# Another order of the PSUM evictions, and another dealing of the projections and linear quarters, in masked attention with an int8 linear layer

## The chip, the cores and the metric

The kernel runs on one core of one Trainium2 chip. The metric is the device time of one execution in microseconds; lower is better. The engines are named as in the profile: PE (TensorE, matmuls), PEld (its weight loads), DVE (VectorE), ACT (ScalarE), POOL (GpSimd), SP (SyncE, which here issues the DMAs).

## The reference

x has the shape 8 x 512 x 1024 (batch, channels, tokens). Attention with 16 heads of width 32 runs over the tokens, and its result, channels by tokens, goes through an int8 linear layer over the token axis; the result is added to x. Cut to what matters:

```
Q, K, V = proj(Wq), proj(Wk), proj(Wv)
att = einsum('bhqd,bhkd->bhqk', Q, K) * (1.0 / sqrt(Dh)) + b[0]
att = att * m + (1.0 - m) * NEG_INF
y = einsum('bhqk,bhkd->bhqd', softmax(att, axis=-1), V)
q, in_scale = per_token_quant_int8(y)        # rows of y: one channel, 1024 tokens
acc = einsum('bsk,nk->bsn', q, weight)       # int8, int32 sums
out = x + (acc * in_scale * w_scale[:, 0] + bias).astype(float16)
```

## The kernel before

**Groups and steps.** Four heads of one batch element make a group: 8 x 4 = 32 groups (i). A group has two halves of 512 queries (X = 2i and 2i + 1), and each half has 8 chunks of 128 keys, so a group has 16 steps, t = 0 to 15, and the kernel 512 steps s. The engines' instructions are in an order written out by hand: the loop at the end (L717 to L775) walks the steps, and each engine runs what it is given in that order.

**One step.** `scores` (L332) gives, for one chunk of keys and 512 queries, the four heads' scores: first a shift by the row's maximum (L343), then the products (L348), into two single PSUM banks and one pair. `exponentials` (L356) has ACT take the exponential in three parts (L362: two singles, then the pair). `add_up` (L365) has POOL add the exponentials of a half over its chunks (L372); for a half's first chunk (t = 0 and t = 8) it issues nothing. `maxima` (L270) computes the scores of queries by keys for a later step, `LEAD` = 11 steps ahead, to find each row's maximum: four products with 32 rows each (L281), for head j = 0 into two single banks, for head j = 1 into a pair. `take_maxima` (L289) has DVE add the mask row and reduce with a custom instruction (L301): two passes over the singles, one pass over the pair, each followed by a short read of its accumulator.

**Banks.** There are eight PSUM banks: four singles (`one`) and two pairs (`two`). `score_banks` and `maxima_banks` (L85 to L93): scores take `two[1]` and, in even steps, `one[0:2]`, in odd steps `one[2:4]`. Maxima take `two[0]` and the two singles that the scores of that step don't take. So the maxima of step s + 1 write the singles that step s used for its scores, and the pair that the maxima of step s used.

**What else PE does in a step.** After the maxima of an even step, `product` (L376) multiplies the exponentials of the last two chunks with V, into `one[0]`; `keep_product` (L384) adds that to y on DVE (L392), or, for the first pair of chunks of a half (t = 2 and 10), copies it on ACT (L390). Then a step has jobs, dealt out by `plan` (L618) and put into one bank: `one[1]` in even steps, `one[2]` in odd ones, as soon as the exponential has read it. The jobs are 24 pieces of 128 columns of the next groups' Q, K and V projections (L186), whose results ACT copies out (L219, L221, L266); four quarters of 256 columns of the linear layer of group i - 2 (L186 too), which DVE scales on the way out (L523); and the sums of the denominators (L398), copied by ACT (L404). In the kernel before, pieces come three at a time in the eight odd steps, linear quarters in steps 4, 6, 8 and 10, sums in 2 and 12.

**What follows a step.** `rest_of` (L667) spreads small work. `normalise` is four reciprocals of the denominators on DVE (L432) and then, as its last part (step number HN = 4), the product of y with them, both in SBUF (L435). For the odd half 2i - 1 it has its parts in steps 5, 6, 6, 7 and 8 of group i, for the even half 2i in steps 13, 14, 14, 15 and step 0 of the next group. `quantise` finds the row's largest value on DVE (L442, L447, L449, part 0, at step 8) and rounds in four ACT passes over y (L479, L481, L483, L485, parts 1 to 4, at steps 10, 12, 14 and 0); `turn` has a DMA transpose the result. `load_residual`, `add_residual` (POOL, L517 and L518) and the store handle the last addition for group i - 2. `split_tops` (POOL, L320 and L322) and a DMA transpose prepare the shifts three steps ahead of a half.

Of the kernel before, what the change touches and what calls it, by code (L numbers as in the profile page):

```python
# [24 lines left out]
LEAD = 11  # L25
# [8 lines left out]
def kernel(  # L34
# [15 lines left out]
    nc = tc.nc  # L50
# [3 lines left out]
    NT = T // P  # L54
    NH = T // HALF
    HN = HALF // P
    n_groups = B * NG
    n_halves = n_groups * NH
    n_steps = n_halves * NT
# [25 lines left out]
    def score_banks(s):  # L85
        a = 0 if s >= TAIL else s % 2
        return one[2 * a : 2 * a + 2], two[1 - s % 2 if s >= TAIL else 1]
# [198 lines left out]
                    stop=True,  # L286
                )

    def take_maxima(m, accs):  # L289
        X, u = divmod(m, NT)  # L290
        pair, n = divmod(u, HN)
        row = masks[X // NH // NG][0]
        if u == 0:
            tops[X] = small.tile([P, HN, HG], F32, tag="tops", name=f"tops_{X}")
        for j in range(2):
            apart = accs[j][0].tensor is not accs[j][1].tensor
            for a in range(NH if apart else 1):
                keys = slice(a * HALF, (a + 1) * HALF if apart else T)
                top = tops[X][:, n, 2 * pair + j : 2 * pair + j + 1]
                rest = work.tile([P, T], BF, tag="rest", name=f"rest_{m}_{j}_{a}")  # L300
                nc.vector.tensor_tensor_reduce(  # L301
                    out=rest[:, keys],
                    in0=accs[j][a] if apart else both(accs[j]),
                    in1=row[:, keys],
                    scale=-1.0,
                    scalar=top if a else HIGH,
                    op0=ALU.add,
                    op1=ALU.min,
                    accum_out=top,
                )  # L310
# [115 lines left out]
    def normalise(X, step):  # L426
        i, h = divmod(X, NH)
        d = dens[X]
        if step < HN:
            cols = slice(step * P, (step + 1) * P)  # L430
            source = one[2] if X == n_halves - 1 else d
            nc.vector.reciprocal(d[:, cols], source[:, cols])  # L432
        else:
            y = ys[i][:, h * HALF : (h + 1) * HALF]
            nc.vector.tensor_tensor(y, y, d, ALU.mult)  # L435
# [55 lines left out]
    def turn(i):  # L491
        _, scale, qt = quants.pop(i)
        qT = work.tile([P, NT, P], BF, tag="qT", name=f"qT_{i}")
        nc.sync.dma_start_transpose(qT, qt)
        outs[i] = qT, scale
# [92 lines left out]
    def group(i):  # L588
        return 0 <= i < n_groups
# [3 lines left out]
    def pieces(what, *args, size=P):  # L593
        multiply, keep = what
        if what is of_v:
            return [(multiply, keep, args, slice(k, k + 1), P) for k in range(NT)]
        return [
            (multiply, keep, args, slice(c, c + size), size) for c in range(0, HALF, size)
        ]
# [18 lines left out]
    def plan(i):  # L618
        if i < 0:
            early = pieces(of_qk, 0, 0, 1) + pieces(of_v, 0) + pieces(of_qk, 1, 0, 0) + pieces(of_qk, 1, 1, 0)  # L620
            return {SG - LEAD + a: early[2 * a : 2 * a + 2] for a in range(len(early) // 2)}
        steps = {}
        if i == last:
            if group(i - 2):
                steps[1] = pieces(of_linear, i - 2, 0)
                steps[3] = pieces(of_linear, i - 2, 1)
            steps[2] = [(*sums_of, (2 * i - 1,), None, HALF)]
            return steps
        k1, v, q1 = pieces(of_qk, i + 1, 1, 1), pieces(of_v, i + 1), pieces(of_qk, i + 1, 0, 1)
        q2 = pieces(of_qk, i + 2, 0, 0) if group(i + 2) else []  # L630
        k2 = pieces(of_qk, i + 2, 1, 0) if group(i + 2) else []
        row = k1 + v + q1 + q2 + k2
        for a in range(NT):
            steps[2 * a + 1] = row[3 * a : 3 * a + 3]
        if group(i - 1):
            steps[2] = [(*sums_of, (2 * i - 1,), None, HALF)]
        steps[12] = [(*sums_of, (2 * i,), None, HALF)]
        if group(i - 2):
            for h in range(NH):
                for a, piece in enumerate(pieces(of_linear, i - 2, h, size=HALF // 2)):  # L640
                    steps[4 + 4 * h + 2 * a] = [piece]
        return steps

    def job(i, t):
        if i not in plans:
            plans.clear()
            plans[i] = plan(i)
        return together(plans[i].get(t, []))
# [18 lines left out]
    def rest_of(i, t):  # L667

        if i == last:
            if t == 5:  # L670
                for step in range(HN):
                    normalise(2 * i - 1, step)
            if t == 6:
                normalise(2 * i - 1, HN)
                quantise(i - 1, 0)
            if t == 7:
                for step in range(1, 4):
                    quantise(i - 1, step)
                turn(i - 1)
            if t == 9:  # L680
                for step in range(HN):
                    normalise(2 * i, step)
            if t == 10:
                normalise(2 * i, HN)
                tops_y.append(largest(i, 0))
                for h in range(NH):
                    load_residual(i - 1, h)
        else:
            late_steps = {5: (0,), 6: (1, 2), 7: (3,), 8: (HN,)}.get(t, ())
            if group(i - 1):  # L690
                for step in late_steps:
                    normalise(2 * i - 1, step)
                if t == 8:
                    quantise(i - 1, 0)
                if t in (10, 12, 14):
                    quantise(i - 1, t // 2 - 4)
                if i == last - 1 and t == 15:
                    quantise(i - 1, 4)
                    turn(i - 1)
            for step in {13: (0,), 14: (1, 2), 15: (3,)}.get(t, ()):  # L700
                normalise(2 * i, step)
        if t == 0 and group(i - 1):
            normalise(2 * i - 2, HN)
            if group(i - 2) and i < last:
                quantise(i - 2, 4)
        if t == 1 and group(i - 2) and i < last:
            turn(i - 2)

    tops_y = []
    load_mask(0)  # L710
# [6 lines left out]
    for s in range(-LEAD, n_steps):  # L717
        i, t = divmod(s, SG)
        if i >= 2:
            h = {0: 0, 2: 1}.get(t) if i == last else {3: 0, 7: 1}.get(t)  # L720
            if h is not None:
                load_residual(i - 2, h)
            h = {2: 0, 4: 1}.get(t) if i == last else {7: 0, 11: 1}.get(t)
            if h is not None:
                add_residual(i - 2, h, nc.gpsimd)
            if t in ((4, 6) if i == last else (9, 13)):
                flush(stores)
        if t in (4, 12):
            flush(casts)
        X, u = divmod(s + 3, NT)  # L730
        if u == 0 and 0 <= X < n_halves:
            split_tops(X)
            place_tops(X)
        items = job(i, t)
        if s >= TAIL:
            items, bank = [], None
        elif s < 0:
            bank = one[2 + s % 2]
        else:
            bank = score_banks(s)[0][1 - s % 2]  # L740
        places = []
        width = 0
        for item in items:
            places.append(bank[:, width : width + item[4]])
            width += item[4]

        def multiply():
            for (what, _, args, cols, _), place in zip(items, places):
                what(*args, cols, place) if cols else what(*args, place)

        if s < 0:
            multiply()
        if s >= 0:
            scores(s)
            exponentials(s)
            add_up(s)
        m = s + LEAD
        if m < n_steps:
            maxima(m, maxima_banks(s))
            take_maxima(m, maxima_banks(s))  # L760
        if s >= TAIL:
            for a in range(ON_ARRAY if s == TAIL + 1 else s - 1, s if s > TAIL else 0):
                late(a)
        elif s > 0 and s % 2 == 0:
            acc = score_banks(s)[0][0]
            for a in (2, 1):
                product(s - a, acc, a == 2, a == 1)
            keep_product((s - 2) // NT, (s - 2) % NT == 0, acc)
        if s >= 0:
            multiply()  # L770
        for (_, keep, args, cols, _), place in zip(items, places):
            keep(*args, cols, place)
        load_ahead(i, t)
        if i >= 0:
            rest_of(i, t)  # L775
# [64 lines left out]
```

## Time and profile before

| what | value |
|---|---|
| median of 3 runs | 2576.94 us (2576.03 to 2578.45) |
| the profiled execution's own time | 2576.91 us |
| its span in the profile | 2575.1 us |
| exponential, 128x512, and 128x1024 (L362) | 684 ns, 1117 ns |
| maxima pass over a single, first and second (L301) | 682 ns, 751 ns |
| maxima pass over the pair (L301) | 1224 ns |
| addition to y (L392) | 682 ns |
| linear quarter's eviction (L523) | 479 ns |
| reciprocal (L432) | 932 ns |
| addition of exponentials on POOL (L372) | 4564 ns |

A row of the profile's groups gives the line, the engine, the operation, what is written and read, how many there are, the busy time in all and the mean of one. In the timeline, a row begins with the start and the duration in us, and brackets at its end give the engine's idle time before it and what ended that. Matmuls of different rows or columns of the array run at the same time, so that their durations overlap.

A step's length is the distance from one step's first shift product (L343) to the next one's in the timeline. For the group that starts at 1231.82 us and ends at 1310.74 us, a steady one, these starts are:

| t | 0 | 1 | 2 | 3 | 4 | 5 | 6 | 7 |
|---|---|---|---|---|---|---|---|---|
| start, us | 1231.82 | 1235.75 | 1241.38 | 1246.17 | 1251.02 | 1255.83 | 1261.01 | 1265.82 |

| t | 8 | 9 | 10 | 11 | 12 | 13 | 14 | 15 |
|---|---|---|---|---|---|---|---|---|
| start, us | 1271.34 | 1276.15 | 1281.29 | 1286.42 | 1291.24 | 1296.04 | 1301.17 | 1305.07 |

Most other groups are 78.57 us long (this one is 0.35 longer, at step 7); groups 0 and 1 take 77.50 and 77.13, group 30 takes 75.07.

### The profile page before, as it was taken

The numbers are of one execution on the slowest core, as the hardware profiler recorded it, in microseconds if no ns is written. First come the engines' busy times: TensorE is split into PE (matmuls) and PEld (weight loads), VectorE is DVE, ScalarE is ACT, GpSimd is POOL, SyncE is SP. The second block draws the span as 40 slices with busy tenths as digits, with TensorE's granted clock in tenths as the row PEclk, the third lists the DMA queues.
The fourth block names the chain that finished last, engine by engine and source line by source line (L and its number), as shares of the span: only waits on it lengthen the run. The fifth ranks groups of instructions, "written<-read, shape, count | busy, mean of one in ns | idle before, by whom it ended". The sixth has DMA issues, their size and how long they took to land.

```text
span 2575.1 us, 80820 instructions
## 1 busy us (share of the span) xinstructions
PE 2502.2 (97%) x35008; PEld 1135.4 (44%) x35008; DVE 1859.3 (72%) x3829; ACT 1524.4 (59%) x2166; POOL 2218.4 (86%) x901
## 2 busy tenths in 40 slices
PE   9999999999999999999999999999999999999997
PEld 4444444444444444444444444444444444444432
DVE  5677677777777776777777777767777777777674
ACT  1556666566666656656566665566655666555654
POOL 0998989889889889898898898898988988988992
PEclk9999999999999999999999999999999999999999
DMA  4012111121111211112111121111211122111111
GB/s 122 20 30 80 43 37 31 49 72 43 41 43 39 73 39 43 37 39 73 39 43 41 51 63 41 39 43 45 63 41 39 46 62 59 30 41 39 35 32 44
DMA packets 143509, 121.37 MB, mean 47 GB/s; under 512 B 74800, under 2 KB 108592, under 8 KB 143152
## 3 DMA queue, kind: packets, MB, share of 16 engines
q1 hardware_dynamic: 143152, 116.20, 16.5%
q8 instruction: 274, 4.49, 0.7%
q14 instruction: 83, 0.68, 0.1%
HBM read 57.70 MB, written 16.78 MB: 29 GB/s over the span
## 4 chain that ended last, share of the span: by engine, by line
PE 86%; DVE 7%; issue 4%; ACT 2%; DMA 0%; POOL 0%; DVEq 0%; SPq 0%; POOLq 0%
PE one L186 31%; PE one L281 17%; PE one L380 14%; PE one L348 13%; PE one L343 5%; DVE rest L301 5%; PE one L398 3%; DVE y L392 2%; PE two L281 2%; ACT e L362 1%; ACT den L404 1%; ACT y L481 1%; DVE tops L301 0%; DMA x<-in_x 0%; PE two L348 0%
## 5 line engine op out<-in xcount | busy, mean ns | idle before, releaser
L372 POOL TENSOR_TENSOR sum<-sum,e 128x2048 f32<-128x2048 f32 x374 | 1706.8, 4564 | 82.8 <-ACT e L362 72.9
L362 ACT ACTIVATE e<-one,kbias 128x512 f32<-128x512 f32 x1024 | 648.4, 684 | 483.1 <-PE two L348 469.7
L301 DVE CUSTOM_DVE_ANT_0 rest<-one,row 128x512 bf16<-128x512 f32 x509 | 347.3, 682 | 505.6 <-PE two L281 295.2
L301 DVE CUSTOM_DVE_ANT_0 rest<-two,row 128x1024 bf16<-128x1024 f32 x515 | 630.2, 1224 | 77.6 <-PE one L281 1.5
L362 ACT ACTIVATE e<-two,kbias 128x1024 f32<-128x1024 f32 x512 | 571.8, 1117 | 0.0
L281 PE MATMUL one<-kf,qf 32*128 32x512 f32 x1022 | 529.1, 597 | 42.0 <-DVE y L392 40.2
L281 PE MATMUL two<-kt,qt 32*128 32x512 f32 x1026 | 544.0, 613 | 0.0
L281 PE MATMUL one<-kt,qt 32*128 32x512 f32 x1014 | 539.9, 612 | 0.0
L281 PE MATMUL two<-kf,qf 32*128 32x512 f32 x1034 | 536.4, 601 | 0.2 <-DVE tops L301 0.2
L348 PE MATMUL one<-qf,kf 32*128 32x512 f32 x2048 | 524.5, 588 | 0.0
L348 PE MATMUL two<-qf,kf 32*128 32x512 f32 x2048 | 523.1, 588 | 0.0
L380 PE MATMUL one<-e,v 128*32 128x512 f32 x4096 | 494.9, 599 | 0.0
L372 POOL TENSOR_TENSOR sum<-e,e 128x2048 f32<-128x2048 f32 x63 | 286.5, 4548 | 199.5 <-ACT e L362 199.5
L301 DVE CUSTOM_DVE_ANT_0 rest<-one,row,tops 128x512 bf16<-128x512 f32 x509 | 382.2, 751 | 74.9 <-DVE tops L301 1.5
L281 PEld LDWEIGHTS one<-kf,qf 32*128 32x128 f32 x1022 | 174.9, 184 | 286.4 <-DVE y L392 161.5
L380 PEld LDWEIGHTS one<-e,v 128*32 128x32 f32 x4096 | 107.8, 109 | 354.7 <-ACT e L362 197.4
L186 PE MATMUL one<-wv,x 128*32 128x128 f32 x8192 | 243.0, 273 | 0.0
L186 PE MATMUL one<-x,wq 128*32 128x256 f32 (+1 forms) x4032 | 237.5, 381 | 5.5 <-ACT e L362 5.5
L186 PEld LDWEIGHTS one<-wv,x 128*32 128x32 f32 x8192 | 220.2, 110 | 50.1 <-ACT e L362 47.0
L186 PE MATMUL one<-x,wk 128*32 128x128 f32 (+2 forms) x3968 | 239.1, 382 | 0.0
L432 DVE RECIPROCAL den<-den 128x128 f32<-128x128 f32 x252 | 229.4, 932 | 0.3 <-ACT den L404 0.3
L343 PE MATMUL one<-shift,ones_b 32*128 32x512 bf16 x1024 | 201.6, 385 | 11.1 <-DVE tops L301 8.3
(88 smaller groups left out, 2809.5 us busy)
## 6 DMA issues: line engine op xcount, KB each, us to landing
x<-in_x SPq DMA_DIRECT2D x32, 512.0 KB, 4.3
qt<-qf SPq DMA_DIRECT2D x128, 128.0 KB, 2.3
xr<-in_x SPq DMA_DIRECT2D x62, 256.0 KB, 3.6
out<-o SPq DMA_DIRECT2D x62, 256.0 KB, 2.3
wk<-in_wkT SPq DMA_DIRECT2D x32, 256.0 KB, 3.2
wq<-in_wqT SPq DMA_DIRECT2D x32, 256.0 KB, 3.5
kt<-kf SPq DMA_DIRECT2D x64, 128.0 KB, 2.3
mask<-in_cond SPq DMA_DIRECT2D x8, 512.0 KB, 4.2
```

What stands on the lines that cost most here:

```text
L186: nc.tensor.matmul(acc[r : r + DH], weights[:, r : r + DH], moving, **kwargs)
L281: nc.tensor.matmul(accs[j][a], q[r : r + DH, n * P : (n + 1) * P], k[r : r + DH, :], start=True, stop=True,)
L301: nc.vector.tensor_tensor_reduce(out=rest[:, keys], in0=accs[j][a] if apart else both(accs[j]), in1=row[:, keys], scale=-1.0, scalar=top i ...
L343: nc.tensor.matmul(accs[j], ones_b[r, :], shift[r, :], start=True, stop=False)
L348: nc.tensor.matmul(accs[j], k[r, k0 * P : (k0 + 1) * P], q[r, :], start=False, stop=True,)
L362: nc.scalar.activation(part, acc, AF.Exp, bias=kbias[:, kc : kc + 1], scale=SCALE)
L372: nc.gpsimd.tensor_tensor(sums[X], other, exps[s], ALU.add)
L380: nc.tensor.matmul(acc[r, :], v_sb[s // SG][:, kc, r], exps[s][:, j, :], start=start, stop=stop)
L392: nc.vector.tensor_tensor(y, y, acc, ALU.add)
L398: nc.tensor.matmul(acc[j * DH : (j + 1) * DH, :], ones_f, term[:, j, :], start=start, stop=stop)
L404: nc.scalar.copy(dens[X], acc)
L432: nc.vector.reciprocal(d[:, cols], source[:, cols])
```

## The change

- `take_maxima` gets a list of heads. In a step from s = 0 on, DVE first takes the two passes over the single banks (head 0). Then stands the eviction of the head product (the addition to y, in even steps) and, in odd steps, that of the linear quarter. Then comes the pass over the pair (head 1). In even steps of the last group a linear eviction follows the pair. ACT's evictions come after that in program order. Before, all three passes came first and the evictions behind them.
- The linear quarters go from steps 4, 6, 8, 10 to steps 3, 5, 7, 9. In such a step they take `one[2]`, and projections take `one[3]`; in other odd steps projections stay in `one[2]`, in even steps in `one[1]`.
- The 24 projection pieces are dealt out over 13 of the 16 steps by a row of counts for t = 0 to 15, 1, 3, 0, 2, 1, 2, 1, 2, 1, 2, 1, 3, 0, 3, 0, 2.
- `normalise` has one part a step: the odd half's at steps 3 to 7, the even half's at 13, 14, 15 and, in the next group, 0 and 1. So L435 goes from steps 8 and 0 to steps 7 and 1.
- `quantise` goes to steps 10 to 14 and `turn` to step 15 of the same group.
- Residual loads go from steps 3 and 7 to 1 and 5, the additions on POOL from 7 and 11 to 8 and 12, the stores from 9 and 13 to 10 and 14. The last group has its own steps for all of these.

```diff
--- before.py
+++ after.py
@@ -286,13 +286,13 @@
                     stop=True,
                 )
 
-    def take_maxima(m, accs):
+    def take_maxima(m, accs, heads):
         X, u = divmod(m, NT)
         pair, n = divmod(u, HN)
         row = masks[X // NH // NG][0]
-        if u == 0:
+        if X not in tops:
             tops[X] = small.tile([P, HN, HG], F32, tag="tops", name=f"tops_{X}")
-        for j in range(2):
+        for j in heads:
             apart = accs[j][0].tensor is not accs[j][1].tensor
             for a in range(NH if apart else 1):
                 keys = slice(a * HALF, (a + 1) * HALF if apart else T)
@@ -622,23 +622,24 @@
         steps = {}
         if i == last:
             if group(i - 2):
-                steps[1] = pieces(of_linear, i - 2, 0)
-                steps[3] = pieces(of_linear, i - 2, 1)
+                steps[3] = pieces(of_linear, i - 2, 0)
+                steps[4] = pieces(of_linear, i - 2, 1)
             steps[2] = [(*sums_of, (2 * i - 1,), None, HALF)]
             return steps
-        k1, v, q1 = pieces(of_qk, i + 1, 1, 1), pieces(of_v, i + 1), pieces(of_qk, i + 1, 0, 1)
-        q2 = pieces(of_qk, i + 2, 0, 0) if group(i + 2) else []
-        k2 = pieces(of_qk, i + 2, 1, 0) if group(i + 2) else []
-        row = k1 + v + q1 + q2 + k2
-        for a in range(NT):
-            steps[2 * a + 1] = row[3 * a : 3 * a + 3]
+        row = pieces(of_qk, i + 1, 1, 1) + pieces(of_v, i + 1) + pieces(of_qk, i + 1, 0, 1)
+        if group(i + 2):
+            row += pieces(of_qk, i + 2, 0, 0) + pieces(of_qk, i + 2, 1, 0)
         if group(i - 1):
             steps[2] = [(*sums_of, (2 * i - 1,), None, HALF)]
         steps[12] = [(*sums_of, (2 * i,), None, HALF)]
         if group(i - 2):
             for h in range(NH):
                 for a, piece in enumerate(pieces(of_linear, i - 2, h, size=HALF // 2)):
-                    steps[4 + 4 * h + 2 * a] = [piece]
+                    steps[3 + 4 * h + 2 * a] = [piece]
+        for t, n in enumerate((1, 3, 0, 2, 1, 2, 1, 2, 1, 2, 1, 3, 0, 3, 0, 2)):
+            if n:
+                steps[t] = steps.get(t, []) + row[:n]
+                row = row[n:]
         return steps
 
     def job(i, t):
@@ -686,25 +687,17 @@
                 for h in range(NH):
                     load_residual(i - 1, h)
         else:
-            late_steps = {5: (0,), 6: (1, 2), 7: (3,), 8: (HN,)}.get(t, ())
             if group(i - 1):
-                for step in late_steps:
-                    normalise(2 * i - 1, step)
-                if t == 8:
-                    quantise(i - 1, 0)
-                if t in (10, 12, 14):
-                    quantise(i - 1, t // 2 - 4)
-                if i == last - 1 and t == 15:
-                    quantise(i - 1, 4)
+                if 3 <= t < 4 + HN:
+                    normalise(2 * i - 1, t - 3)
+                if 10 <= t < 15:
+                    quantise(i - 1, t - 10)
+                if t == 15:
                     turn(i - 1)
-            for step in {13: (0,), 14: (1, 2), 15: (3,)}.get(t, ()):
-                normalise(2 * i, step)
-        if t == 0 and group(i - 1):
-            normalise(2 * i - 2, HN)
-            if group(i - 2) and i < last:
-                quantise(i - 2, 4)
-        if t == 1 and group(i - 2) and i < last:
-            turn(i - 2)
+            if t >= 13:
+                normalise(2 * i, t - 13)
+        if t < 2 and group(i - 1):
+            normalise(2 * i - 2, t + 3)
 
     tops_y = []
     load_mask(0)
@@ -717,13 +710,12 @@
     for s in range(-LEAD, n_steps):
         i, t = divmod(s, SG)
         if i >= 2:
-            h = {0: 0, 2: 1}.get(t) if i == last else {3: 0, 7: 1}.get(t)
-            if h is not None:
-                load_residual(i - 2, h)
-            h = {2: 0, 4: 1}.get(t) if i == last else {7: 0, 11: 1}.get(t)
-            if h is not None:
-                add_residual(i - 2, h, nc.gpsimd)
-            if t in ((4, 6) if i == last else (9, 13)):
+            for h in range(NH):
+                if t == ((1, 2) if i == last else (1, 5))[h]:
+                    load_residual(i - 2, h)
+                if t == ((5, 6) if i == last else (8, 12))[h]:
+                    add_residual(i - 2, h, nc.gpsimd)
+            if t in ((7, 8) if i == last else (10, 14)):
                 flush(stores)
         if t in (4, 12):
             flush(casts)
@@ -731,45 +723,59 @@
         if u == 0 and 0 <= X < n_halves:
             split_tops(X)
             place_tops(X)
-        items = job(i, t)
-        if s >= TAIL:
-            items, bank = [], None
-        elif s < 0:
-            bank = one[2 + s % 2]
-        else:
-            bank = score_banks(s)[0][1 - s % 2]
+        items = job(i, t) if s < TAIL else []
+        if s < 0:
+            bank = [one[2 + s % 2]] * 2
+        else:
+            bank = score_banks(s)[0] if s % 2 else score_banks(s)[0][1:] * 2
+        turned_out = [item for item in items if item[1] is keep_linear]
         places = []
         width = 0
         for item in items:
-            places.append(bank[:, width : width + item[4]])
+            if turned_out and item not in turned_out:
+                places.append(bank[1][:, width : width + item[4]])
+            else:
+                places.append(bank[0][:, width : width + item[4]])
             width += item[4]
 
         def multiply():
             for (what, _, args, cols, _), place in zip(items, places):
                 what(*args, cols, place) if cols else what(*args, place)
 
+        def keep(linears):
+            for (_, what, args, cols, _), place in zip(items, places):
+                if (what is keep_linear) == linears:
+                    what(*args, cols, place)
+
+        m = s + LEAD
         if s < 0:
             multiply()
-        if s >= 0:
+            keep(False)
+            maxima(m, maxima_banks(s))
+            take_maxima(m, maxima_banks(s), range(2))
+        else:
             scores(s)
             exponentials(s)
             add_up(s)
-        m = s + LEAD
-        if m < n_steps:
-            maxima(m, maxima_banks(s))
-            take_maxima(m, maxima_banks(s))
-        if s >= TAIL:
-            for a in range(ON_ARRAY if s == TAIL + 1 else s - 1, s if s > TAIL else 0):
-                late(a)
-        elif s > 0 and s % 2 == 0:
-            acc = score_banks(s)[0][0]
-            for a in (2, 1):
-                product(s - a, acc, a == 2, a == 1)
-            keep_product((s - 2) // NT, (s - 2) % NT == 0, acc)
-        if s >= 0:
+            if m < n_steps:
+                maxima(m, maxima_banks(s))
+                take_maxima(m, maxima_banks(s), (0,))
+            if s >= TAIL:
+                for a in range(ON_ARRAY if s == TAIL + 1 else s - 1, s if s > TAIL else 0):
+                    late(a)
+            elif s > 0 and s % 2 == 0:
+                acc = score_banks(s)[0][0]
+                for a in (2, 1):
+                    product(s - a, acc, a == 2, a == 1)
+                keep_product((s - 2) // NT, (s - 2) % NT == 0, acc)
             multiply()
-        for (_, keep, args, cols, _), place in zip(items, places):
-            keep(*args, cols, place)
+            if s % 2:
+                keep(True)
+            if m < n_steps:
+                take_maxima(m, maxima_banks(s), (1,))
+            if s % 2 == 0:
+                keep(True)
+            keep(False)
         load_ahead(i, t)
         if i >= 0:
             rest_of(i, t)
```

## The prediction

> **What bounds the kernel now.** I read the page's parts 1 and 4 first, then the list of waits, then the timeline of one steady group (1231.82 to 1310.74 us), and last the rows of single DVE lines.
>
> ```profile
> PE 2502.2 (97%) x35008; PEld 1135.4 (44%) x35008; DVE 1859.3 (72%) x3829; ACT 1524.4 (59%) x2166; POOL 2218.4 (86%) x901
> ...
> PE 86%; DVE 7%; issue 4%; ACT 2%; DMA 0%; POOL 0%; DVEq 0%; SPq 0%; POOLq 0%
> ```
> ```profile
> PEld one L281 <- DVE y L392: 161.5, 186, 1.8
> ```
>
> PE sets the end, but the chain leaves it for DVE, mostly at the maxima (L281), which wait for the addition to y (L392). The timeline of step 0 shows how. I call M the start of a step's first maxima product.
>
> ```profile
> 1232.90 0.59 PE L281 MATMUL one<-kf,qf 32*128 32x512 f32 x1
> ...
> 1233.90 1.92 PE L380 MATMUL one<-e,v 128*32 128x512 f32 x16
> 1233.95 0.69 DVE L301 CUSTOM_DVE_ANT_0 rest<-one,row 128x512 bf16<-128x512 f32 x1 [0.61 <-PE two L281]
> 1234.80 0.75 DVE L301 CUSTOM_DVE_ANT_0 rest<-one,row,tops 128x512 bf16<-128x512 f32 x1
> 1235.70 1.22 DVE L301 CUSTOM_DVE_ANT_0 rest<-two,row 128x1024 bf16<-128x1024 f32 x1
> ...
> 1236.85 0.68 DVE L392 TENSOR_TENSOR y<-y,one 128x512 f32<-128x512 f32 x1
> ...
> 1237.59 0.69 PE L281 MATMUL one<-kf,qf 32*128 32x512 f32 x1 [0.58 <-DVE y L392]
> ```
>
> DVE starts at M+1.05, reaches y at M+3.95, and the next M is M+4.69; PE alone could do this step in 3.94. PE's pieces by the same timeline: fixed part with one head product 3.94; a projection piece 0.90; a linear quarter or the sums 0.87; three pieces 2.75. So a full step is 4.80 to 4.83 and a group's PE floor is 2 x 3.92 + 14 x 4.81 = 75.2 against 78.57 measured. The 3.4 us of waits lie in steps 1 and 15 (0.83 each, after the bare even steps), 5, 7, 9 (0.38 each, where the linear eviction follows y), 10 and 13 (0.33 each; at 13 the copy of den and a quantise pass hold the exponential).
>
> **The change, step by step.**
>
> *Even steps with y (0, 4, 6, 8, 12, 14).* y now stands ahead of the pass over the pair. It needs the head product: its start M+1.00 plus 1.99 (product at 1243.46, ACT's copy of it at 1245.45 to 1245.51). DVE's two single passes end at about M+2.66, so DVE idles to M+2.99. Then y 0.61 to the next start, the paired pass 1.22, and 0.07 to the waiting product: M+4.89 for the bank pair. What queues behind the waiting y is that paired pass and the reciprocal; the next step's maxima wait for it. With one projection piece PE needs 4.83, so 4.89 counts, in steps 0, 4, 6 and 8. Step 10 copies y on ACT: 4.83; step 2: 4.80.
>
> *Odd steps.* The linear quarter (0.87) plus two pieces is 4.80, three pieces 4.82. The quarter's eviction starts at about M+2.6, when its products, done by M+1.9, are long there; the paired pass ends at M+4.2, and a reciprocal (0.95) still ends before the next M+1.05. So the 0.38 in 5, 7, 9 goes. Quantise's first part (1.5 us) at step 10 lies behind a pass that ends at M+4.03 and is done before M+5.9: free. The residual's loads, additions and stores move by one or two steps; POOL and SP have that much time: free, and at most one addition (2.45 us of POOL) late if not.
>
> *ACT.* Quantise 1 to 4 now follow evictions in steps 11, 12 and 13. After an eviction begins 0.13 behind the shift, an exponential is due at 1.35. Step 11: 0.13 + 0.48 + 1.14 - 1.35 = 0.40 late; step 12: 0.32 (as measured today); step 13: 0.13 + 0.54 + 1.05 - 1.35 = 0.37. The exponential releases the bank that PE writes next, so step 12 becomes 5.29, 13 5.05, and 14 with 15 (two pieces, DVE's chain) 9.15. A new mask's passes now also stand behind evictions: 2 x 0.33 in seven groups, 4.6 in all. From zero to double is possible for these: -1.1 to +1.1 us a group.
>
> Sum of a group: 4 x 4.89 + 4.83 + 4.80 + 2 x 4.82 + 4 x 4.80 + 5.29 + 5.05 + 9.15 = 77.52, **1.05 less** than 78.57.
>
> *What is moved with it: the product of y with the reciprocals (L435).* It goes from steps 0 and 8, where add_up issues nothing on POOL, to steps 1 and 7, where POOL adds exponentials (L372, 4.56 us each). The row of L435 has one odd value, and the timeline explains it:
>
> ```profile
> L435 DVE TENSOR_TENSOR y<-y,den x64: 678/682/3224, 138.2 to 2556.6; 128x512 f32<-128x512 f32 x64
> ```
> ```profile
> 2490.99 4.56 POOL L372 TENSOR_TENSOR sum<-sum,e 128x2048 f32<-128x2048 f32 x1
> ...
> 2492.88 3.22 DVE L435 TENSOR_TENSOR y<-y,den 128x512 f32<-128x512 f32 x1
> ...
> 2495.50 4.97 POOL L372 TENSOR_TENSOR sum<-e,e 128x2048 f32<-128x2048 f32 x1
> 2496.03 0.68 DVE L301 CUSTOM_DVE_ANT_0 rest<-one,row 128x512 bf16<-128x512 f32 x1
> ```
>
> L435 ended 0.55 after the addition that was running, and the next addition took 4.97 instead of 4.54. At 138.24 the same: the addition (134.46 + 4.55) had 0.77 to go, and L435 took 1.33. In the steady groups L435 now starts within 0.15 us of an addition's end, which is why it shows 0.68. L392, with one input in PSUM, is 0.68 in all 188 runs beside the same additions. So an L435 that meets an addition lasts what remains of it plus 0.55.
>
> Step 1: the addition starts when the exponential ends, M+2.67, and runs to M+7.21. L435 comes at M+3.96 and ends at M+7.75; the next single pass should begin at M+5.88. It begins 1.8 late, its paired pass ends at M+10.65, and the maxima of step 3 are at M+10.70 instead of M+9.62: **1.08 lost**.
>
> Step 7: POOL runs without a break from step 4 (start M4+2.67; 4.57, then the splitting 1.46, then two additions of 4.61), so addition 6 ends at M4+17.9, which is M7+3.4, since M7 = M4 + 14.5; addition 7 runs to M7+7.97. L435 comes at M7+4.17 and ends at M7+8.5, that is M8+3.7. Step 8 then: passes at 3.65 and 4.50, y 5.18, paired pass 5.79 to 7.01, next maxima at M8+7.08 instead of 4.89: **2.19 lost**. Bounds for the two together: nothing (L435 at an addition's end, as today) and a whole addition each, 2 x 4.56 less the 1.8 that a step's DVE slack takes off each, 5.5.
>
> A rule of the Trainium skill bears on this: SBUF — State Buffer, "Who interferes with whom", says that a VectorE instruction with two SBUF inputs and a GpSimd one that reads SBUF exclude each other, and the second waits until the first has finished. By it L435 would last the remainder plus its full 0.68, not 0.55: 0.13 more per meeting, some 8 us over 60.
>
> *The sum.* 28 steady groups (2 to 29): 77.52 + 1.08 + 2.19 - 0.06 (step 8's wait, already counted) = 80.73 against 78.57, +2.16 each, +60.5. Group 0 has neither linear quarters nor L435 in these steps: -3.3. Group 1, without linear, 74.7 + 3.27 against 77.13: +0.9. Group 30: 75.0 + 3.27 against 75.07: +3.2. Group 31, where L435's 3.22 us at step 0 goes and comes back at step 1: -2.4. Masks +4.6; waits of 0.35 that five groups show now, -1.8. Together +61.7 on the profiled execution, 2576.91 (span 2575.1 and 1.8 around it; the median of the runs is 2576.94): **2638 us**. With the steady group uncertain by 1 us, 2610 to 2668.
>
> **Rivals.**
>
> *Faster: L435 isn't held.* If its meetings cost nothing, each of 30 groups loses 3.27 less: 2638 - 98 = **2540**. For it: 61 of 64 L435 show 0.68 today, and the phase of POOL at step 7 is a sum of ten terms. Against it: at step 1 the addition starts 1.3 us ahead of L435 whatever the phase, and both old meetings that overlapped were held. The change turns to a gain when the meetings cost under 1.1 us a group instead of 3.27, a third.
>
> *Half held.* If addition 6 ended 0.8 later, L435 of step 7 would slip in ahead of addition 7: 2638 - 30 x 2.19 = **2572**, about no change. If only step 1 were free: 2606.
>
> *A lower clock as well.* After the held L435 of 2492.88, PE stood still for 0.77, 0.53 and 0.79 us within 4 us, and the granted clock fell:
>
> ```profile
> 2500.00:2505.00 5.00, 5.00 (x32) 0.98 (x29) 2.69 (x6) 1.73 (x3) 4.92 (x4) 0.69 0.14 52
> ```
>
> That is half speed for some 3.4 us, 1.7 us of work. Step 8 will have 1.4 us of such gaps within 3.3, a little less than there. If each group fell once: 2638 + 30 x 1.7 = **2689**. TensorE: Matmul & The Clock Gate, "Part 1", has the clock fall after an idle window of about 3.4 us; by that no gap here is long enough and nothing is added. The row above speaks against taking it so strictly.
>
> *The change doesn't do what it says.* In bare even steps y ahead of the pair is no earlier release: 4.89 against 4.69, since DVE waits for the head product. That is in the sum already.
>
> **Chances.** Forecast 0.62; lower clock too 0.12; half held 0.10 (half of it at 2572, half at 2606); not held 0.16. The range leaves out the last and a tail: 2572 to 2692. A difference below 0.2%, about 5 us, can't be told from none. Faster is 0.16 and most of the 2572 half, 0.19; within 0.2%, 0.04; slower 0.77.
>
> **What will show it.** Right: L435's median rises to 3 us or more with the additions beside it; steps 2 and 8 are about 5.9 and 7.1 us; steps 5, 7, 9 fall to 4.8; the wait of L281 for L392 gives way to one for the paired pass. Wrong: L435 still at 0.68, so that steps 2 and 8 stay under 5; or steps 4 and 6 well above 4.9, where y's wait for the head product was taken too small; or half clock in the steady groups.

## The result, and the profile after

The changed kernel takes 2635.98 us (2634.02 to 2636.84, 4 runs) against 2576.49 us for the kernel before: 1.0228 times as long, 95% interval 1.0211 to 1.0246. The forecast was 2638.

The page of the changed kernel, parts 1 and 4:

```profile
PE 2572.1 (98%) x36000; PEld 1210.1 (46%) x36000; DVE 2040.1 (78%) x3829; ACT 1539.5 (58%) x2259; POOL 2230.7 (85%) x901
...
PE 75%; issue 11%; DVE 9%; ACT 4%; DMA 0%; POOL 0%; DVEq 0%; SPq 0%; POOLq 0%
```

With as many instructions as before, DVE is busy for 180.8 us more, and the chain runs over PE for less of the span. The row of L435, min/median/max in ns, and the timeline around step 8:

```profile
L435 DVE TENSOR_TENSOR y<-y,den x64: 691/3742/4150, 139.6 to 2615.4; 128x512 f32<-128x512 f32 x64
```
```profile
1296.22 4.55 POOL L372 TENSOR_TENSOR sum<-sum,e 128x2048 f32<-128x2048 f32 x1
...
1297.24 4.09 DVE L435 TENSOR_TENSOR y<-y,den 128x512 f32<-128x512 f32 x1
1300.73 1.72 POOL L517 TENSOR_TENSOR o<-o,bias_sb 128x512 f16<-128x512 f32 x1
1301.25 0.68 DVE L301 CUSTOM_DVE_ANT_0 rest<-one,row 128x512 bf16<-128x512 f32 x1
...
1302.89 0.37 PE L343 MATMUL one<-shift,ones_b 32*128 32x512 bf16 x1 [0.53 <-DVE tops L301]
```

L435 starts 1.0 us after the addition, ends 0.56 after that addition's end at 1300.77, the next POOL instruction takes 1.72 instead of 1.28, and PE waits for the passes that stood behind L435.

The other new wait stands in step 0 of the same group, in the place of the one that was removed:

```profile
1258.07 0.59 PE L281 MATMUL one<-kf,qf 32*128 32x512 f32 x1
...
1259.07 1.92 PE L380 MATMUL one<-e,v 128*32 128x512 f32 x16
...
1261.13 0.69 DVE L392 TENSOR_TENSOR y<-y,one 128x512 f32<-128x512 f32 x1 [0.40 <-PE one L380]
1261.73 1.22 DVE L301 CUSTOM_DVE_ANT_0 rest<-two,row 128x1024 bf16<-128x1024 f32 x1
...
1262.89 0.59 PE L281 MATMUL one<-kf,qf 32*128 32x512 f32 x1
...
1263.02 0.69 PE L281 MATMUL two<-kf,qf 32*128 32x512 f32 x1
1263.09 0.18 PEld L281 LDWEIGHTS one<-kt,qt 32*128 32x128 f32 x1
...
1264.18 2.79 PE L186 MATMUL one<-x,wk 128*32 128x384 f32 x32
```

DVE stands idle 0.40 for the head product. The pair is free at 1262.95, and its product starts 0.13 after the single's. But the next work starts 1.29 after the single's product, where an undisturbed step needs 1.00 (1258.07 to 1259.07): the weights behind the waiting product were loaded only after it.

Where the time lies by step, in the kernel before, the changed one and the experiments, shows best in the steps' lengths (us, means over groups 2 to 29, from each timeline's shift products):

| t | before | changed | l435_back | quantise_ahead | y_behind_pair | all_three | l435_on_pool |
|---|---|---|---|---|---|---|---|
| 0 | 3.94 | 4.81 | 4.81 | 4.81 | 5.05 | 5.05 | 5.03 |
| 1 | 5.63 | 5.11 | 5.11 | 5.11 | 4.80 | 4.80 | 4.80 |
| 2 | 4.80 | 4.81 | 4.81 | 4.81 | 4.81 | 4.81 | 4.81 |
| 3 | 4.84 | 5.60 | 4.83 | 5.61 | 5.94 | 4.83 | 4.78 |
| 4 | 4.81 | 4.81 | 4.81 | 4.81 | 4.81 | 4.81 | 4.81 |
| 5 | 5.19 | 5.13 | 5.12 | 5.13 | 4.91 | 4.91 | 4.91 |
| 6 | 4.81 | 4.82 | 4.82 | 4.82 | 4.82 | 4.82 | 4.81 |
| 7 | 5.20 | 5.02 | 5.02 | 5.02 | 4.85 | 4.85 | 4.85 |
| 8 | 4.81 | 4.95 | 4.81 | 4.96 | 5.34 | 4.81 | 4.81 |
| 9 | 5.13 | 6.51 | 5.09 | 6.51 | 7.33 | 4.85 | 4.86 |
| 10 | 5.14 | 4.81 | 4.81 | 4.81 | 4.81 | 4.81 | 4.81 |
| 11 | 4.82 | 4.79 | 4.79 | 4.79 | 4.79 | 4.79 | 4.79 |
| 12 | 4.80 | 5.19 | 5.19 | 4.80 | 5.19 | 4.80 | 4.80 |
| 13 | 5.14 | 5.14 | 5.14 | 5.13 | 5.14 | 4.89 | 4.04 |
| 14 | 3.90 | 4.30 | 4.30 | 3.90 | 4.30 | 3.90 | 4.93 |
| 15 | 5.68 | 5.02 | 5.03 | 5.02 | 4.41 | 4.81 | 3.96 |
| group | 78.63 | 80.82 | 78.49 | 80.03 | 81.29 | 76.54 | 75.78 |

### The profile page after: what moved, and what is told of

Its sections match the earlier page's. It is cut to its first block, busy times and chain, and to the rows that moved or that the text cites. A ratio compares the mean times of both kernels' runs of the same rounds, so it can differ in the third digit from the quotient of the medians.

```text
span 2632.2 us, 82631 instructions
## 1 busy us (share of the span) xinstructions
PE 2572.1 (98%) x36000; PEld 1210.1 (46%) x36000; DVE 2040.1 (78%) x3829; ACT 1539.5 (58%) x2259; POOL 2230.7 (85%) x901
## 4 chain that ended last, share of the span: by engine, by line
PE 75%; issue 11%; DVE 9%; ACT 4%; DMA 0%; POOL 0%; DVEq 0%; SPq 0%; POOLq 0%
PE one L186 23%; PE one L380 14%; PE one L348 13%; PE one L281 11%; DVE rest L301 8%; PE two L281 6%; PE one L343 5%; PE one L398 2%; ACT e L362 2%; ACT qf L219 1%; ACT y L483 1%; ACT y L479 1%; DVE o L523 0%; DVE tops L301 0%; PE two L348 0%
## 5 line engine op out<-in xcount | busy, mean ns | idle before, releaser
L281 PE MATMUL two<-kf,qf 32*128 32x512 f32 x1034 | 548.2, 613 | 0.3 <-DVE tops L301 0.2
L348 PE MATMUL one<-qf,kf 32*128 32x512 f32 x2048 | 537.3, 592 | 0.0
L281 PE MATMUL one<-kf,qf 32*128 32x512 f32 x1022 | 521.9, 590 | 0.0
L281 PEld LDWEIGHTS one<-kf,qf 32*128 32x128 f32 x1022 | 187.3, 185 | 191.5 <-issue 118.7
L186 PE MATMUL one<-wv,x 128*32 128x128 f32 x8192 | 252.1, 273 | 0.0
L343 PE MATMUL one<-shift,ones_b 32*128 32x512 bf16 x1024 | 222.9, 384 | 26.5 <-DVE tops L301 20.8
L186 PE MATMUL one<-x,wq 128*32 128x128 f32 (+2 forms) x5024 | 248.3, 338 | 0.0
L186 PEld LDWEIGHTS one<-wv,x 128*32 128x32 f32 x8192 | 226.5, 110 | 44.9 <-issue 37.9
L435 DVE TENSOR_TENSOR y<-y,den 128x512 f32<-128x512 f32 x64 | 239.3, 3739 | 0.2
L186 PE MATMUL one<-x,wk 128*32 128x256 f32 (+2 forms) x3968 | 239.0, 382 | 0.0
```

Of the source, the lines that this page charges most:

```text
L186: nc.tensor.matmul(acc[r : r + DH], weights[:, r : r + DH], moving, **kwargs)
L281: nc.tensor.matmul(accs[j][a], q[r : r + DH, n * P : (n + 1) * P], k[r : r + DH, :], start=True, stop=True,)
L343: nc.tensor.matmul(accs[j], ones_b[r, :], shift[r, :], start=True, stop=False)
L348: nc.tensor.matmul(accs[j], k[r, k0 * P : (k0 + 1) * P], q[r, :], start=False, stop=True,)
```

## The experiments

Theory 1: L435 is held by POOL's additions, which makes the change slow. Rivals: the new order among the passes, ACT's late quantise passes, or something else in L435's step. Medians are given, and ratios to the kernel before on the same chip with their 95% intervals.

**l435_back**: L435 in steps 8 and 0.

```diff
-                if 3 <= t < 4 + HN:
-                    normalise(2 * i - 1, t - 3)
+                if 3 <= t < 3 + HN or t == 8:
+                    normalise(2 * i - 1, min(t - 3, HN))
...
-        if t < 2 and group(i - 1):
-            normalise(2 * i - 2, t + 3)
+        if t == 0 and group(i - 1):
+            normalise(2 * i - 2, HN - 1)
+            normalise(2 * i - 2, HN)
```

> The changed kernel with one part undone: L435 stands in steps 8 and 0 again, where POOL adds no exponentials. Theory 1 (L435 is held by the additions): L435's median falls from 3.74 us to about 0.7, step 3 from 5.60 to 4.8 and step 9 from 6.51 to about 4.9, 2.5 to 2.7 us a group, so 2636 less 75 to 95: 2541 to 2561, faster than the kernel before. Rival (the order of the evictions or ACT's late passes make the change slow): 2620 to 2636.

Measured 2570.29 us, 0.9976 (0.9967 to 0.9986): 65.7 less than the changed kernel, under the expected 75 to 95. Step 3 goes from 5.60 to 4.83, steps 8 and 9 together from 11.46 to 9.90. The held L435 is what makes the change slow; without it the rest is worth 5.7 us.

```profile
L435 DVE TENSOR_TENSOR y<-y,den x64: 689/693/2430, 136.2 to 2550.1; 128x512 f32<-128x512 f32 x64
```

**before_l435_moved**: the kernel before, L435 alone in steps 7 and 1.

```diff
-            late_steps = {5: (0,), 6: (1, 2), 7: (3,), 8: (HN,)}.get(t, ())
+            late_steps = {5: (0,), 6: (1, 2), 7: (3, HN)}.get(t, ())
...
-        if t == 0 and group(i - 1):
-            normalise(2 * i - 2, HN)
-            if group(i - 2) and i < last:
-                quantise(i - 2, 4)
+            if group(i - 2) and i < last:
+                quantise(i - 2, 4)
+        if t == 1 and group(i - 1):
+            normalise(2 * i - 2, HN)
```

(The quantise part stays in step 0.)

> The kernel before with L435 alone moved: from steps 8 and 0 to steps 7 and 1, behind that step's reciprocal. Theory 1: L435 again lasts what is left of the addition that runs, 2 to 4.6 us each; at step 7 it comes after a reciprocal and just behind the start of an addition, so up to 4 us are lost there and about 0.3 at step 1 (where the old wait for y leaves slack): 2660 to 2720. Rival (L435's place doesn't matter without the new order): 2577.

Measured 2729.65 us, 1.0596 (1.0579 to 1.0614), just above the range. The timeline of the odd half's L435, and the window behind it (length, then PE, PEld, DVE, ACT and POOL busy, then the granted clock, DMA share and GB/s):

```profile
1257.74 4.57 POOL L372 TENSOR_TENSOR sum<-sum,e 128x2048 f32<-128x2048 f32 x1
...
1257.94 4.92 DVE L435 TENSOR_TENSOR y<-y,den 128x512 f32<-128x512 f32 x1
...
1263.52 0.37 PE L343 MATMUL one<-shift,ones_b 32*128 32x512 bf16 x1 [2.23 <-DVE tops L301]
```
```profile
1266.00:1270.00 4.00, 3.60 (x20) 1.35 (x24) 3.53 (x8) 1.92 (x3) 2.00 (x1) 0.57 0.00 0
```

L435 comes 0.2 us after an addition's start and takes 4.92. PE waits 2.23 at a stretch, and here the lower clock comes as well: once in each of the groups 1 to 30 the granted clock falls to half, for 3.4 us (in three groups 6.8). By the cost of such a fall in y_behind_pair below, 1.56 us a group, some 47 of the 154 us lost are the clock's (an estimate). So the hold doesn't need the new order.

**pool_writes**: the changed kernel; the expectation says what it leaves out.

```diff
-        nc.gpsimd.tensor_tensor(sums[X], other, exps[s], ALU.add)
+        if kc in (1, NT - 1):
+            nc.gpsimd.tensor_tensor(
+                sums[X][:, :, :8], other[:, :, :8], exps[s][:, :, :8], ALU.add
+            )
+            nc.gpsimd.memset(sums[X][:, :, 8:], 1.0)
+        else:
+            nc.gpsimd.tensor_tensor(sums[X], other, exps[s], ALU.add)
```

> The changed kernel, L435 left in steps 1 and 7. For the second and the last chunk of a half, POOL adds only 8 of the 512 columns and fills the rest of the sum with ones, a memset that reads nothing; so the denominators leave most of these two chunks out. Theory 1 (POOL's reading beside L435 is what holds it): L435 runs beside the memset at about 0.7 us, and as in l435_back the kernel loses some 65 us against the changed one: 2565 to 2580. Rival A (any POOL work on SBUF holds it): L435 lasts what is left of the memset plus 0.55, 1 to 2 us. Rival B (what holds L435 is not POOL but something of its step): L435 stays at 3.7 us and the time at 2636.

Measured 2566.63 us, 0.9967 (0.9955 to 0.9978), 69.4 less than the changed kernel. L441 is L435 here:

```profile
1235.07 1.78 POOL L376 MEMSET sum<- 128x2016 f32 x1
1236.23 0.69 DVE L441 TENSOR_TENSOR y<-y,den 128x512 f32<-128x512 f32 x1
```
```profile
L441 DVE TENSOR_TENSOR y<-y,den x64: 682/686/3009, 139.6 to 2545.7; 128x512 f32<-128x512 f32 x64
```

L435 starts in the middle of the memset, which runs to 1236.85, and takes 0.69; what was left of the memset plus 0.55 would be 1.17. All 59 that met a memset took 0.68 or 0.69. The one of 3.01 met an addition that reads, with 2.46 to go. Step and place are those of the changed kernel; what is gone is POOL's reading beside it. Both rivals fall. The Trainium skill, SBUF — State Buffer, "Who interferes with whom", states just that, contention with a GpSimd instruction that reads SBUF and not with one that only writes it; this run agrees (0.69 beside the memset, 3.74 beside the addition).

**quantise_ahead**: ACT's quantise passes ahead of its copies. These lines stand in the loop in front of `keep(False)` and no longer in `rest_of`:

```diff
+            if i < last and group(i - 1) and 10 <= t < 15:
+                quantise(i - 1, t - 10)
             keep(False)
```

> The changed kernel with ACT's quantise passes issued ahead of the copies of the projections in the same step. Theory: in steps 11 to 13 these passes stand behind a copy that waits for PE, and so hold the next exponential by 0.3 to 0.4 us; ahead of it they fill the time in which ACT waits. Steps 12 and 13 fall from 5.19 and 5.14 to 4.8, step 14 with 15 by 0.3: 1.0 us in each of 29 groups, 2600 to 2610. Rival (ACT is not what ends there): 2636.

Measured 2612.09 us, 1.0142 (1.0127 to 1.0157), 23.9 less than the changed kernel and just above the expected range. The timeline of step 12 into 13 there:

```profile
1310.47 1.16 ACT L481 ACTIVATE y<-y,rounding 128x1024 f32<-128x1024 f32 x1
...
1311.90 0.59 ACT L404 COPY den<-one 128x512 f32<-128x512 f32 x1 [0.28 <-PE one L398]
1313.11 1.27 ACT L362 ACTIVATE e<-one,kbias 128x512 f32<-128x512 f32 x2 [0.62 <-PE two L348]
```

The pass runs while ACT would wait for the sums, and the exponential waits for PE again, not for ACT. Steps 12 and 14 lose 0.4 each. Step 13 stays at 5.13, against expectation: as all_three shows, it is an odd step behind an even one with y, and waits for the pair like steps 1 and 5.

**y_behind_pair**: y behind the pass over the pair in even steps.

```diff
+                if m < n_steps:
+                    take_maxima(m, maxima_banks(s), (1,))
                 keep_product((s - 2) // NT, (s - 2) % NT == 0, acc)
...
-            if m < n_steps:
+            if m < n_steps and (s % 2 or s == 0):
                 take_maxima(m, maxima_banks(s), (1,))
```

> The changed kernel with the addition to y put behind the pass over the pair again in even steps; the linear quarters' eviction stays ahead of the pair in odd steps. Theory: y ahead of the pair costs, because it waits for the head product (0.4 us of idle DVE) and the pair is free only at M+4.95, while PE could go on at M+4.83; behind the pair, y is done at M+4.64. Steps 1, 5 and 7 lose their 0.2 to 0.3 each and step 15 about 0.2: 2636 less 20 to 35, 2601 to 2616. Rival (y ahead of the pair is the useful part of the change, as it frees a single bank early): 2640 or more.

Measured 2645.89 us, 1.0277 (1.0262 to 1.0292): slower, a miss. Steps 1, 5, 7 and 15 got shorter as expected, by 0.31, 0.22, 0.17 and 0.61; but the steps behind a held L435 got longer, step 3 by 0.34 and steps 8 and 9 by 1.21, and step 0 by 0.24. And the clock fell in 10 of the 28 steady groups, in step 9:

```profile
497.00:501.00 4.00, 3.27 (x35) 1.45 (x36) 1.69 (x6) 2.27 (x3) 1.64 (x1) 0.59 0.19 70
```

These 10 groups take 82.29 us in the mean. The other 18 take 80.73, a little less than the changed kernel's 80.82: in them y, which now stands behind everything that L435 delays, costs 0.32 in step 3, 0.62 in steps 8 and 9 and 0.24 in step 0, about what the other steps gain. So what makes this run the slower one is the lower clock, 10 times 1.56 us. Whether y's place is good can't be judged beside a held L435. So the parts were put together:

**l435_back_quantise_ahead**: both edits of these names.

> The changed kernel with L435 in steps 8 and 0 and the quantise passes ahead of ACT's copies; y stays ahead of the pair. Both gains should add: 2570 less 24, 2540 to 2550; step 12 at 4.80, 14 at 3.90. If the quantise passes only hid behind the held L435, 2565 or more.

Measured 2546.54 us, 0.9886 (0.9871 to 0.9901): the two gains add up (65.7 and 23.7).

**all_three**: the same with y behind the pair.

> As the one before, with y behind the pair in even steps too. Theory: y_behind_pair was slower only because its later end adds to the steps in which L435 is held (steps 3, 8, 9, and the lower clock in some groups); its steps 1, 5, 7, 15 were 0.3, 0.2, 0.2, 0.6 shorter. Without held L435 it should now gain about 2 us a group over the one before: 2485 to 2510. Rival (y ahead of the pair is better by itself): 2550 or more.

Measured 2512.55 us, 0.9753 (0.9739 to 0.9768), just above the expected range. Step 13 falls to 4.89 and step 9 to 4.85. So y ahead of the pair, the change's own first idea, costs 34.0 us here; in the kernel with a held L435 it looked 9.9 better, by way of the clock.

**linear_behind**: all_three with the linear eviction behind the pair as well.

```diff
-            if s % 2:
-                keep(True)
             if m < n_steps and (s % 2 or s == 0):
                 take_maxima(m, maxima_banks(s), (1,))
-            if s % 2 == 0:
-                keep(True)
+            keep(True)
```

> As all_three, with the linear quarters' eviction behind the pair in the odd steps too, so that no eviction stands between the passes and only the dealing of the jobs is left of the change. Theory: the gain in steps 5, 7, 9 comes from the quarters standing in odd steps, where DVE has 0.7 us to spare, not from the place among the passes; the later eviction ends at M+4.5, before the next M at M+4.8: the same as all_three, 2505 to 2520. Rival (the place among the passes is what frees PE): 0.3 us in three or four steps of a group, 2540 or more.

Measured 2513.81 us, 0.9754 (0.9739 to 0.9768): the same. The eviction's place among the passes is worth nothing; that the quarters stand in odd steps is enough.

**all_three_dealt**: all_three with one piece moved from step 13 to 14.

```diff
-(1, 3, 0, 2, 1, 2, 1, 2, 1, 2, 1, 3, 0, 3, 0, 2)
+(1, 3, 0, 2, 1, 2, 1, 2, 1, 2, 1, 3, 0, 2, 1, 2)
```

> As all_three, with one projection piece moved from step 13 to step 14, so that no even step of a steady group is left without a job: a bare even step is bounded by DVE at 4.69 while PE needs 3.94. Steps 13, 14 and 15 together should fall by 0.3 to 0.6: 8 to 18 us below all_three. Rival (PE's total alone decides): the same time as all_three.

Measured 2510.01 us, 0.9745 (0.9730 to 0.9759), 2.5 less instead of 8 to 18. Steps 13 to 15 fell from 13.60 to 13.05, as expected; but L435 came earlier against POOL's queue, lasted 1.8 at step 0 instead of 1.2, and step 2 rose from 4.81 to 5.30.

**l435_on_pool**: all_three_dealt with L435 on POOL.

```diff
-            nc.vector.tensor_tensor(y, y, d, ALU.mult)
+            engine = nc.gpsimd if X < 2 * last - 1 else nc.vector
+            engine.tensor_tensor(y, y, d, ALU.mult)
```

> As all_three_dealt, with the product of y and the reciprocals (L435) moved from DVE to POOL, in steps 8 and 0; only the last halves keep it on DVE. In all_three_dealt L435 still lasts 1.6 us by the median, because a tail of an addition or of the residual's additions runs beside it, and step 2 is 5.30. On POOL it stands in one queue with the additions, 1.2 us each. Theory: step 2 falls to 4.8 and a group by 0.4 to 0.6, 2490 to 2500. Rival (POOL is too full: 14 additions of 4.6, 5 us of residual, 3 of splitting and now 2.4 are 74.9 of a group's 76.4, so that the sums or shifts come late): 2510 or more.

Measured 2486.00 us, 0.9644 (0.9628 to 0.9661), below the expected range: the best version, 90.9 us under the kernel before. L435 takes 1.28 us on POOL, and step 2 falls from 5.30 to 4.81. Its page:

```profile
PE 2458.9 (99%) x36959; PEld 1173.1 (47%) x36960; DVE 1819.5 (73%) x3768; ACT 1550.6 (62%) x2289; POOL 2293.3 (92%) x962
...
PE 97%; DVE 1%; ACT 1%; issue 0%; DMA 0%; POOL 0%; SPq 0%; POOLq 0%; DVEq 0%
```

POOL carries it, at 92%, and nearly all of the chain is PE. A group is 75.78, 0.6 above the PE floor of 75.2.

## Why the prediction was right, and where it wasn't

The time (2638 against 2635.98) and the mechanism were right: L435 is held, and the steps behind it (3, 8 and 9 in the table) rose, though less than forecast. But two terms were wrong in size and nearly cancelled, so that a miss of under 3 us is in large part luck: the holds were put 32 us too high, the rest of the change 27 too low (0.91 a group in 30). In part the two are one error, since waits that the second term left out lie under the holds.

- **L435 held.** Its durations were predicted well: 3.79 and 4.35 against 3.74 and 4.12. All 61 that met an addition ended 0.55 or 0.56 after its end, as the prediction took it from two rows, and not 0.68, as by the rule that it quotes. The cost of the two was 3.27 a group in the sum, 98 us in 30 groups; l435_back shows 65.7. By the table it is 0.77 (step 3) and 1.56 (steps 8 and 9), 2.33 a group. From M to M, as the prediction counts, steps 2 and 8 are 5.24 and 5.85, not 5.9 and 7.1, and some of the loss comes only in steps 3 and 9 (5.17 and 5.62). For the hold in step 1 the reason can be read off, from the changed kernel's timeline:

```profile
1266.84 3.72 DVE L435 TENSOR_TENSOR y<-y,den 128x512 f32<-128x512 f32 x1
...
1272.22 1.22 DVE L301 CUSTOM_DVE_ANT_0 rest<-two,row 128x1024 bf16<-128x1024 f32 x1
...
1273.51 0.69 PE L281 MATMUL two<-kf,qf 32*128 32x512 f32 x1
```

The maxima of step 3 write the pair 10.62 after step 1's M (1262.89), close to the 10.70 of the forecast. But without the hold they would do so at 9.92 (steps 1 and 2 take 5.11 and 4.81 in l435_back), not at 9.62: step 1 is late already by y's wait. Step 9 would have its own 0.29, which the sum took for 0.06. The rest of what steps 8 and 9 lost less than forecast was not followed up.

- **The rest of the change.** The step that failed is the term for the even steps with y: "4.89 counts, in steps 0, 4, 6 and 8", 0.06 above PE's 4.83 each. The time at which the product into the pair starts was close (M+4.95 measured, 1263.02 in the rows above with M at 1258.07; M+4.89 forecast). But the loss is 0.31, 0.33, 0.22 and, in l435_back, 0.29 in the four odd steps that follow (5, 7 and 9 were to fall to 4.8), 1.15 together instead of 0.24; steps 4 and 6, where the prediction looked for it, are 4.81 and 4.82. With y behind the pair, in all_three, 0.21 of it stays, so some 0.9 is y's. Two things were left out. DVE sees the head product 2.06 after its start, in 154 of 157 waits, not 1.99; ACT's copies show 1.99 in about half and 2.05 in the others, among them the row that the prediction read (1243.46 to 1245.51). And a product that waits holds the weight loads behind it. With that, the forecast gain of 1.05 a group shrinks to 0.14 (78.63 to 78.49), and the 2540 of the rival without holding would have been 2570. The waits themselves changed as forecast: that of the maxima for L392 fell from 161.5 us, and one for the pass over the pair came up (us in total, times, longest):

```profile
PEld two L281 <- DVE tops L301: 44.7, 73, 1.1
...
PEld one L281 <- DVE y L392: 24.4, 64, 0.5
```

- **ACT's late passes.** Step 12 came out at 5.19 (forecast 5.29), 14 and 15 together at 9.32 (9.15), 13 at 5.14 (5.05). quantise_ahead shows that ACT is the reason for 12 and 14. For 13 it isn't: there the size was right by luck, for another reason, y's wait. The 4.6 us for a new mask's passes didn't come: all groups from 2 to 29, with a new mask or without, take 80.77 to 80.85 us.
- **Linear quarters in odd steps.** The 0.38 behind them did go, all but 0.05 to 0.11, as linear_behind and all_three show (steps 5, 7, 9 at 4.85 to 4.91). In the changed kernel y's wait stands in its place.
- **The lower clock** didn't come in the steady groups of the changed kernel, where PE is busy for at least 81% of every 3.4 us. It did come in before_l435_moved, where PE waits 2.2 us at a stretch, and in y_behind_pair, which differs by one exchange in DVE's order. That rival was near.

## What to carry to other kernels

Before an instruction is moved on one engine, look up what the other engines run at that moment: 61 products of 0.68 us on VectorE, which took no longer than that where they met at most the end of a GpSimd addition, cost 66 us of the kernel's time in the middle of GpSimd's additions, though no wait in the program ties them together. An eviction put earlier frees its bank earlier only if its data are there; otherwise the in-order engine waits with all that stands behind it. And when a change of many parts comes out slow, undo the parts one by one and then together: here y's new place looked good or bad according to whether L435 was held.

## What the runs showed that was not expected

The granted clock of PE fell to half for 3.4 us behind windows without any long gap. In y_behind_pair PE's longest gap in the 3.4 us before a fall was 0.73 us, with two or three gaps of 0.53 to 0.73 in it and PE busy for 48 to 60% of the window; in the steady groups of the kernel before, where no window was under 0.7 busy, it never fell. Not every window like that was followed by a fall: in y_behind_pair four of 57 to 60%, on the same 3.4 us grid, were not; and in the last group of the changed kernel it fell behind one of 76%. So the share alone doesn't settle it, and what does stays open. The Trainium skill, TensorE: Matmul & The Clock Gate, "Part 1", speaks of an idle window; these runs show that a half-idle one can do it.

A wait of 0.13 us at one product of the maxima cost 0.3 us of the step, since the weight loads behind it didn't run ahead. That this is all of the difference was not shown by itself.
